# A gated cross-attention and quantized FFN block: quantized tokens transposed on TensorE, a new prologue, another order at the end of block 7, and block 1's queries from transposed tokens in DRAM

## The chip, the core and the metric

One core of one Trainium2 chip runs the program. The metric is the device time of one execution in microseconds. TensorE is called PE here, its weight loads PEld, VectorE DVE, ScalarE ACT, GpSimd POOL, and SyncE, which issues nearly all DMAs, SP. Every engine executes its own instructions in order.

## The reference

There are 2 x 2048 tokens of width 512, a context of 77 tokens for each of the two batches, and 16 heads of width 32. The FFN has 2048 hidden values and rounds its operands to integers, with one scale for a whole tensor.

```python
x = x + tanh(g_xattn) * xattn(layernorm(x), ctx)       # softmax(q k^T / sqrt(32)) v, then Wo, bo
x = x + tanh(g_ffn) * ffn(layernorm(x))

def quant(x):                       # per tensor
    scale = max(max(abs(x)), 1e-6) / 127
    return round(x / scale), scale
def qlinear(x, w, b):
    xq, sx = quant(x); wq, sw = quant(w)
    return (xq @ wq.T + b) * (sw * sx)
ffn(x) = qlinear(gelu(qlinear(x, w1, b1)), w2, b2)
```

## The kernel before

The 4096 tokens are eight blocks of 512 (`TB`), each of four tiles of 128; blocks 0 to 3 belong to batch 0. All eight blocks of x stay in SBUF (`X[i]`). The program has three stages: attention over all blocks, in fp32 (0 to 396 us of the profile); the first product of the FFN over all blocks, in bf16 integers (to 509 us); and the second product (to the end).

**Order.** In the attention the order of every engine's instructions, SP's included, is the order of the program's text (`manual_schedule`). In the first FFN product this holds for PE alone; a scheduler places the rest.

**Attention.** A block has four groups of four heads, and runs in eight steps `s`; a step takes one group and two tiles (`part` gives which). `scores` of a step are made on PE (L528) two steps ahead; DVE takes the maxima (`mx`, L537), ACT the exponentials (`e`, eight instructions, L548); DVE sums (`sm`, L562) and inverts (`rs`), POOL multiplies (`e`, L566), PE transposes (`pta`, L577), ACT copies (`aT`), PE multiplies with V (`pc`, L586; L605 in block 7) and ACT copies (`cT`). Queries of block 0 and 1 come from `project_q` (`pq`, L353), those of later blocks and all output projections from 7 units of products of quarters (`qa`, `qb`, `oa`, `ob`, L443), whose sums of quarters POOL makes (`wq_s`, `wo_t`, `xt`, `cs`, L380). Work of neighbouring blocks is spread over the steps by the tables `begin`, `second`, `plan` and `end`; `at(k, task)` puts a task at the end of global step k = 8 i + s.

**Prologue.** For block 0, x is loaded by tiles; DVE takes statistics and normalizes (`xn`, L335), POOL makes the inverse deviation (`rstd`, L174 and L175), PE transposes (`ptx`, L344), ACT copies (`xnT`). PE projects K by groups (`pk`, L236); DVE places each group in a block matrix (`place_k`: four instructions, with ACT taking half of them in batch 1). `nbk`, a scaled bias that only batch 1 uses, is made on POOL from the load `bk_sb`. `pk`, `pq`, `pvv` (V) and `pm` alternate between two PSUM banks (`bank`), in the order of the text.

**Queries.** In block 1 the tokens are normalized and transposed as in block 0 (steps 2 to 4). From block 2 on, `xT`, a copy of x that is transposed in DRAM, is loaded instead (`load_xT`); POOL multiplies it by a row of rstd (`scale_x`, L306), and Wq has had the mean of its rows taken off (`center_wq`, after `sum_columns`), which does what subtracting the mean of the tokens would. The row goes through DRAM: SP writes it (`write_row`, L293), waits for it and reads it as a row on all partitions (`read_row`, L299).

**Block 7** takes the half of tiles 0 and 1 for all groups first (steps 0 to 3), then the half of tiles 2 and 3 group by group, so that the output projections of tiles 2 and 3 (`project_o`, L621) end only with the last group. The scale of the FFN's input needs the extremes of all rows (`extreme`, L647, on DVE); after it the chain goes over `pg_x` to `xqT0`, the quantized, transposed tokens of block 0.

**First product.** For each block, 16 chunks of hidden values in four tiles `G`: four matmuls of 128x512 each (`ph`, L1031), gelu on ACT (L1039), and a maximum over each two chunks on DVE (`hmax`, L1049). `quantize_x` makes the tokens of the next block: DVE normalizes four tiles, multiplies and rounds in two passes of half a block (`quantize`, L211 and L212), and SP transposes each tile by a DMA:

```python
nc.sync.dma_start_transpose(xqT[:, :, r], xq[:, t, :])      # L1010, four per block
```

22 of the 32 tiles G are written to DRAM, 10 are held. The second product (L1098) follows when the last maximum gave its scale.

Of the kernel before, what the change touches and what calls it, by code (L numbers as in the profile page):

```python
# [42 lines left out]
def tile_flamingo_gated_block(  # L43
# [88 lines left out]
    for g in range(2, NG):  # L132
        load_group(nc.sync, wq_sb, wqT, g)
    for b in range(1, B):
        load_ctx(nc.sync, b)
    load_x(1)
# [5 lines left out]

    nc.sync.dma_start(wo_sb, kchunks(woT))
# [10 lines left out]
    nc.vector.memset(ones, 1.0)  # L154
    mhalf = const.tile([P, NT], F32, name="mhalf")
# [6 lines left out]
    hmax = const.tile([P, NB * GT * 2 + 1], F32, name="hmax")  # L162
# [55 lines left out]
    with actx:  # L218
# [97 lines left out]
        def sum_columns(total):  # L316

            pm = bank("pm")
            nc.tensor.matmul(pm, ones, total, start=True, stop=True)
            mean = work.tile([P, D], F32, tag="rrow", name="wq_mean", bufs=1)  # L320
            nc.scalar.activation(mean, pm, AF.Copy, scale=1.0 / D)
            return mean
# [27 lines left out]
        def project_q(i, g):  # L350
            pq = bank(f"pq{i}_{g}")
            for kc in range(KC):
                nc.tensor.matmul(  # L353
                    pq,
                    wq_sb[:, kc, g * P : (g + 1) * P],
                    (xnT if i < 2 else xT_sb)[i][:, kc, :],
                    start=(kc == 0),
                    stop=(kc == KC - 1),
                )
# [153 lines left out]
        def part(i, s):  # L513


            return divmod(s, 2) if i + 1 < NB else (s % NG, s // NG)

        def scores(i, s):

            g, half = part(i, s)  # L520
# [3 lines left out]
            for u in range(2):  # L524
                t = 2 * half + u
# [71 lines left out]
        def apply_v_half(i, s):  # L597

            g, half = part(i, s)
            odd = s % 2  # L600
            pc = ps_t.tile([P, H], F32, tag="pt", name=f"pc{i}_{s}")
            for j in range(HG):
                r = slice(j * DK, (j + 1) * DK)
                c = g * P + j * DK
                nc.tensor.matmul(  # L605
                    pc[r, :],
                    vblk[i // NBB][:, c : c + DK],
                    aT[i, s // 2][:, j, odd * H : (odd + 1) * H],
                    start=True,
                    stop=True,  # L610
                )
            if s in (0, 2):
                cT[i, g // 2] = work.tile([P, 2, TB], F32, tag="cT", name=f"cT{i}_{g}", bufs=3)
            nc.scalar.copy(cT[i, g // 2][:, g % 2, half * H : (half + 1) * H], pc)
# [135 lines left out]
        begin = {1: ("", "p2"), 3: ("", "p3"), 5: ("", "P0"), 6: ("", "P1"), 7: ("", "P2")}  # L750
# [25 lines left out]
        nbk = small.tile([P, KC], F32, tag="nbk", name="nbk", bufs=1)  # L776
        nc.gpsimd.tensor_scalar(nbk, bk_sb, -SCALE, None, ALU.mult)
# [27 lines left out]
        for i in range(NB):  # L805
# [3 lines left out]
            for s in range(2 * NG):  # L809
# [22 lines left out]
                if i == 0:  # L832
# [7 lines left out]
                    if s in (5, 6):  # L840
                        for n in range(2):
                            sums_wq(2 * (s - 5) + n)
# [5 lines left out]
                if i > 0 and s < 2:  # L848
                    for n in ((1, 2), (4,))[s]:
                        sums_c(i - 1, n)  # L850
                if more and i > 0:
# [5 lines left out]
                for t in range(NT):  # L857
                    if s == ((4, 5, 6, 7) if i == 0 else (4, 4, 5, 6))[t]:
# [15 lines left out]
                if i > 0:  # L874
# [4 lines left out]
                    these = {5: (0,), 6: (1,), 7: (2,)} if more else {6: (0, 1), 7: (2,)}  # L879
# [11 lines left out]
                if not more and s > 4:  # L891

                    if s < 7:
                        project_o(i, s - 5)
                        later = [(add_o, i, s - 5), (norm2_stats, i, s - 5)]
                    else:
                        both = ps_s.tile([P, NR, 512], F32, tag="ps", name="po_last")
                        for these in (0, 1), (2,):
                            project_o(i, 2, these)
                            for n, c in enumerate(halves):  # L900
                                project_o(i, 3, these, c, psum=both[:, n, :])
# [12 lines left out]
                for task, args in tasks.get(k, ()):  # L914
                    task(*args)
                if i + 2 < NB:
# [8 lines left out]
        i, last = NB - 1, range(NG - 1, NG)  # L925
# [4 lines left out]
        project_o(i, 2, last)  # L930
        for c in halves:
            project_o(i, 3, last, c)
        for n in range(3, 2 * NT):
            extreme(i - 1, n)
        for t in range(2):
            norm2_max(i, t)
        add_o(i, 2)
        norm2_stats(i, 2)
        norm2_max(i, 2)
# [50 lines left out]
    with ExitStack() as fctx:  # L990
# [3 lines left out]
        )  # L994

        def quantize_x(i):

            xqT = xqT0
            if i % 2:
                xqT = fwork.tile([P, KC, TB], BF16, tag="xqT", name=f"xqT{i}", bufs=1)  # L1000
            n = NT // 2
            for t0 in range(0, NT, n):
                xs = fwork.tile([P, n, D], F32, tag="xs", name=f"xs{i}_{t0}")
                xq = fwork.tile([P, n, D], BF16, tag="xq", name=f"xq{i}_{t0}")
                for t in range(n):
                    normalize2(xs[:, t, :], i, t0 + t)
                quantize(xq, xs, inv_x)
                for t in range(n):
                    r = slice((t0 + t) * P, (t0 + t + 1) * P)
                    nc.sync.dma_start_transpose(xqT[:, :, r], xq[:, t, :])  # L1010
            return xqT

        fctx.enter_context(tc.manual_schedule(engines={mybir.EngineType.PE}))
        for i in range(NB):
            cur = xqT if i else xqT0
            if i + 1 < NB:
                with tc.issue_after(last):
                    xqT = quantize_x(i + 1)
            for a in range(GT):
                G = gtile(f"G{i}_{a}")  # L1020
                for v in range(GF // 2):
# [24 lines left out]
                    k = (i * GT + a) * 2 + v  # L1046
                    n = 1 if k == NB * GT * 2 - 1 else 2
                    for u in range(0, 2, n):
                        nc.vector.tensor_reduce(  # L1049
                            hmax[:, k + u : k + u + 1],  # L1050
                            G[:, 2 * v + u : 2 * v + u + n, :],
# [136 lines left out]
```

## Time and profile before

| | |
|---|---|
| Time, median of 3 runs | 631.1 us (630.91 to 632.41) |
| The profiled execution | 631.38 us, its span 629.5 us |
| Mean granted clock of PE | 0.991 |
| DMA | 94.95 MB, mean 151 GB/s |
| Attention, first product, second product | 0 to 396.4, 396.4 to 508.7, 513.2 to 626.3 us |

Times in the profile count from the start of the span. An instruction's duration is its own; matmuls are pipelined, so the distance between their starts is what counts, and that is what the chain of waits shows. "x8" counts instructions; an fp32 matmul is two, an fp32 transpose one.

### The profile page before, as it was taken

Reading aid. Unit: us, or ns where it says so; the run is one execution under the profiler, and the core shown is the slowest. Engines: PE = TensorE matmul, PEld = TensorE weight load, DVE = VectorE, ACT = ScalarE, POOL = GpSimd, SP = SyncE. Lnnn points to the kernel's source line nnn. Section 1 sums busy time; section 2 is a strip of 40 time slices with the busy share of each in tenths; the row PEclk is TensorE's granted clock in tenths of the full one; section 3 lists DMA queues with packets and bytes.
Section 4 is the critical chain, followed back from the end, with each engine's and each line's share of the span. In section 5 each row is a group of like instructions: output and inputs, shape, how many; then the busy total and the mean of one; then the engine's idle time right before and its main releaser. Section 6 shows DMA issues by size and latency. Waiting matters only on the chain.

```text
span 629.5 us, 9452 instructions
## 1 busy us (share of the span) xinstructions
PE 596.9 (95%) x3322; PEld 370.1 (59%) x3322; DVE 478.3 (76%) x743; ACT 411.3 (65%) x926; POOL 330.6 (53%) x291
## 2 busy tenths in 40 slices
PE   3999999899999999999999997899999979999997
PEld 3556467677778777777777744344444424444444
DVE  4476658668998788778666868999999789877452
ACT  1377556777766867866766653698999879555620
POOL 3076687679777799697885462000000009997000
PEclk9999999999999999999999999799999989999999
DMA  9910350041360053240000040399998019798932
GB/s 288 374 54 1 135 133 18 1 151 67 134 218 1 18 180 124 84 168 1 17 1 1 2 151 0 108 334 342 342 345 232 1 60 376 272 367 320 399 127 83
DMA packets 51270, 94.95 MB, mean 151 GB/s; under 512 B 22219, under 2 KB 26571, under 8 KB 45464
## 3 DMA queue, kind: packets, MB, share of 16 engines
q1 hardware_dynamic: 50120, 93.67, 43.6%
q10 hardware_dynamic: 1104, 0.69, 0.4%
q8 instruction: 26, 0.43, 0.3%
q14 instruction: 20, 0.16, 0.2%
HBM read 57.11 MB, written 33.57 MB: 144 GB/s over the span
## 4 chain that ended last, share of the span: by engine, by line
PE 80%; DVE 9%; ACT 4%; POOL 4%; issue 1%; DMA 1%; ACTq 0%; POOLq 0%; DVEq 0%
PE ph L1031 18%; PE pf L1098 17%; PE pta L577 8%; PE oa L443 6%; PE ps L528 5%; PE qa L443 5%; PE ob L443 5%; PE qb L443 4%; PE pc L586 3%; PE pq L353 3%; ACT e L548 2%; PE po L621 2%; PE pvv L261 1%; POOL cs L380 1%; DVE sm L562 1%
## 5 line engine op out<-in xcount | busy, mean ns | idle before, releaser
L566 POOL TENSOR_TENSOR e<-e,rs 128x616 f32<-128x616 f32 x64 | 77.8, 1216 | 95.7 <-DVE rs L564 89.3
L548 ACT ACTIVATE e<-ps,mx 128x77 f32<-128x77 f32 x512 | 116.9, 343 | 9.9 <-DVE mx L537 9.7
L1098 PE MATMUL pf<-w2q,hq 128*128 128x512 bf16 (+1 forms) x528 | 112.4, 376 | 2.5 <-DVE hq L212 2.3
L1031 PE MATMUL ph<-xqT,w1q 128*128 128x512 bf16 x512 | 112.4, 383 | 1.8 <-DVE xqT L212 1.8
L1039 ACT ACTIVATE G<-ph,b1s,s 128x512 f32<-128x512 f32 x128 | 99.2, 777 | 13.6 <-PE ph L1031 2.9
L578 ACT COPY aT<-pta 77x512 f32<-77x512 f32 x128 | 68.8, 587 | 53.4 <-PE pta L577 53.4
L1098 PEld LDWEIGHTS <-hq 128*128 128x128 bf16 x528 | 51.8, 98 | 63.0 <-DVE hq L212 3.1
L1031 PEld LDWEIGHTS <-w1q 128*128 128x128 bf16 x512 | 50.5, 99 | 63.6 <-issue 4.3
L1049 DVE TENSOR_REDUCE hmax<-G 128x1 f32<-128x1024 f32 (+1 forms) x65 | 76.9, 1197 | 7.0 <-ACT G L1039 6.9
L577 PE MATMUL pta<-ident,e 128*77 128x128 f32 x512 | 71.2, 281 | 2.9 <-POOL e L566 1.3
L1089 POOL TENSOR_SCALAR b_sb<-b_sb,s 128x512 f32<-128x512 f32 x1 | 3.5, 3493 | 122.1 <-issue 122.1
L562 DVE TENSOR_REDUCE sm<-e 128x8 f32<-128x616 f32 x64 | 50.4, 787 | 22.7 <-ACT e L548 22.5
L537 DVE TENSOR_REDUCE mx<-ps 128x8 f32<-128x616 f32 x64 | 50.2, 785 | 22.7 <-PE ps L528 22.5
L1091 ACT ACTIVATE Gb<-Gb,inv_h 128x2048 f32<-128x2048 f32 x22 | 43.6, 2000 | 31.9 <-DMA Gb<-h 30.8
L577 PEld LDWEIGHTS pta<-ident,e 128*77 128x77 f32 x512 | 55.5, 147 | 14.8 <-issue 8.0
L528 PEld LDWEIGHTS ps<-kb,qT 64*128 64x128 f32 x512 | 36.0, 186 | 37.1 <-issue 31.4
L1112 POOL TENSOR_TENSOR x<-x,b_sb 128x512 f32<-128x512 f32 x32 | 57.2, 1825 | 0.1
L528 PE MATMUL ps<-kb,qT 64*128 64x154 f32 x512 | 50.6, 317 | 0.7 <-DVE qT L489 0.4
L1120 DVE SCALAR_TENSOR_TENSOR x<-pf,s,x 128x512 f32<-128x512 f32 (+1 forms) x33 | 23.7, 729 | 34.6 <-PE pf L1098 26.8
L647 DVE TENSOR_REDUCE xm<-x 128x1 f32<-128x512 f32 x64 | 40.8, 669 | 0.0
L348 POOL TENSOR_TENSOR x<-x,bo_sb 128x512 f32<-128x512 f32 x32 | 40.4, 1272 | 0.0
L1092 DVE TENSOR_SCALAR hq<-Gb 128x2048 bf16<-128x2048 f32 x22 | 36.5, 1701 | 1.2 <-ACT Gb L1091 1.1
(146 smaller groups left out, 939.9 us busy)
## 6 DMA issues: line engine op xcount, KB each, us to landing
h<-G SPq DMA_DIRECT2D x22, 1024.0 KB, 5.2
Gb<-h SPq DMA_DIRECT2D x22, 1024.0 KB, 7.8
out_y<-x SPq DMA_DIRECT2D x31, 256.0 KB, 3.1
x<-in_x SPq DMA_DIRECT2D x7, 1024.0 KB, 6.9
xT<-in_xT SPq DMA_DIRECT2D x6, 1024.0 KB, 9.0
raw_w<-in_w2T SPq DMA_DIRECT2D x6, 1024.0 KB, 6.6
raw_w<-in_w1T SPq DMA_DIRECT2D x4, 1024.0 KB, 12.5
w_dram<-xqT SPq DMA_DIRECT2D x4, 512.0 KB, 3.3
```

The costliest lines, as they stand in the source:

```text
L443: nc.tensor.matmul(ps[:, m * H : (m + 1) * H], a[:, c, m * P : (m + 1) * P], b[:, c, :], start=(m + c == 0 and not more), stop=(m + c == 2 ...
L528: nc.tensor.matmul(ps[:, q, u * RK : (u + 1) * RK], qT[i, g // 2][r, g % 2, t * P : (t + 1) * P], kblk[i // NBB][r, g, :], start=True, sto ...
L548: last = nc.scalar.activation(es[i, s][:, u, j * NK : (j + 1) * NK], sc[:, q, u, r, :], AF.Exp, bias=mx[:, q, u, r : r + 1], scale=-1.0,)
L562: nc.vector.tensor_reduce(sm, e4, AX.X, ALU.add)
L566: return nc.gpsimd.tensor_tensor(e4, e4, rs[:, :, :, None].to_broadcast([P, 2, HG, NK]), ALU.mult).ins
L577: nc.tensor.transpose(pt[:NK, j, :], es[i, s][:, u, j, :], ident)
L578: nc.scalar.copy(aT[i, g][:, :, t * P : (t + 1) * P], pt[:NK, :, :])
L1031: nc.tensor.matmul(ph[u], w1q[:, kc, fc * P : (fc + 1) * P], cur[:, kc, :], start=(kc == 0), stop=(kc == KC - 1),)
L1039: nc.scalar.activation(G[:, 2 * v + u, :], ph[u], AF.Gelu, bias=b1s[:, fc : fc + 1], scale=s1,)
L1049: nc.vector.tensor_reduce(hmax[:, k + u : k + u + 1], G[:, 2 * v + u : 2 * v + u + n, :], AX.XY, ALU.max, apply_absolute_value=True,)
L1098: nc.tensor.matmul(po[t, c.start][:, : c.stop - c.start], hq[:, fc, t * P : (t + 1) * P], w2q[:, fc, c], start=(fc == 0), stop=(fc == FC - 1),
L1112: nc.gpsimd.tensor_tensor(y, y, b2_sb, ALU.add)
```

## The change

`quantize_x` no longer transposes by DMA. DVE folds the scale into one pass (`rq`) and rounds in one more; PE transposes the bf16 tiles by `ident16` ahead of the matmuls of tiles a = 2 and a = 3 (`transpose_q`, 8 transposes each), and ACT copies the first half, DVE the second. There is one maximum for each G but the last.

In the prologue 24 transposes of the identity are put ahead of and behind the first transposes, `nbk` goes behind the normalization, K's groups 1 to 3 are placed after the first two scores, and the loads of x1 and the new xT1 come earlier; the fourth piece of w1 is loaded at step 5. Block 1 takes its queries from `xT`: its row is written at step 1, `center_wq` moves from step 3 to step 2, `scale_x` stands at step 3, and all of batch 1's K and V come in steps 3 and 4. Additions of bo (`add_bias`) in blocks 0 and 1 and a sum of Wq move to later steps.

In block 7 the second half goes by tiles: steps 4 and 5 take tile 2, 6 and 7 tile 3, each with two groups. The eight extremes of block 6 move from the end to steps 4 and 5.

```diff
+    load_x(1)
     for g in range(2, NG):
         load_group(nc.sync, wq_sb, wqT, g)
     for b in range(1, B):
         load_ctx(nc.sync, b)
-    load_x(1)
+    load_xT(1)
     nc.sync.dma_start(wo_sb, kchunks(woT))
...
+    ident16 = const.tile([P, P], BF16, name="ident16")
+    nc.vector.tensor_copy(ident16, ident)
...
-        def part(i, s):
-            return divmod(s, 2) if i + 1 < NB else (s % NG, s // NG)
+        def part(i, s, u):
+            if i + 1 < NB:
+                return s // 2, 2 * (s % 2) + u
+            return (s, u) if s < NG else (2 * (s % 2) + u, s // 2)
...
-        begin = {1: ("", "p2"), 3: ("", "p3"), 5: ("", "P0"), 6: ("", "P1"), 7: ("", "P2")}
+        begin = {1: ("", "p2"), 2: ("", "p3"), 5: ("", "P0"), 6: ("", "P1"), 7: ("", "P2")}
...
-        nbk = small.tile([P, KC], F32, tag="nbk", name="nbk", bufs=1)
-        nc.gpsimd.tensor_scalar(nbk, bk_sb, -SCALE, None, ALU.mult)
+        run_up = ps_s.tile([P, KC, P], F32, tag="ps", name="run_up")
+        for n in range(21):
+            nc.tensor.transpose(run_up[:, n % KC, :], ident, ident)
         pk = {}
         for t in range(NT + 1):
...
                 normalize(0, t - 1)
                 transpose_x(0, t - 1)
+            if t == 1:
+                for n in range(3):
+                    nc.tensor.transpose(run_up[:, n, :], ident, ident)
             if t in (2, 3):
                 pk[t - 2] = project_k(0, t - 2)
+        nbk = small.tile([P, KC], F32, tag="nbk", name="nbk", bufs=1)
+        nc.gpsimd.tensor_scalar(nbk, bk_sb, -SCALE, None, ALU.mult)
         place_k(0, 0, pk[0])
-        pk[2] = project_k(0, 2)
-        place_k(0, 1, pk[1])
         project_q(0, 0)
-        place_k(0, 2, pk[2])
-        pk[3] = project_k(0, 3)
-        place_k(0, 3, pk[3])
         load_x(2)
-        for j in range(4):
+        for j in range(3):
             load_w("w1", j)
+        at(5, load_w, "w1", 3)
         for s in range(2):
             scores(0, s)
             exponential(0, s)
+        place_k(0, 1, pk[1])
+        for g in range(2, NG):
+            place_k(0, g, project_k(0, g))
         project_q(0, 1)
...
+                    if s == 3:
+                        for kc in range(KC):
+                            scale_x(1, kc)
...
-                    if s == ((4, 5, 6, 7) if i == 0 else (4, 4, 5, 6))[t]:
+                    if s == ((5, 5, 6, 6) if i == 0 else (5, 6, 6, 7) if i == 1 else (4, 4, 5, 6))[t]:
                         add_bias(i, t)
...
-                if i == 0 and s in (2, 3):
-                    normalize(1, 2 * s - 4)
-                    normalize(1, 2 * s - 3)
...
-                    these = {5: (0,), 6: (1,), 7: (2,)} if more else {6: (0, 1), 7: (2,)}
+                    these = {5: (0,), 6: (1,), 7: (2,)} if more else {4: (0, 1, 2, 3), 5: (4, 5, 6, 7)}
                     for n in these.get(s, ()):
                         extreme(i - 1, n)
...
                 if i == 0 and s == 2:
-                    mean = sum_columns(total)
-                if i == 0 and s == 3:
-                    center_wq(mean)
+                    center_wq(sum_columns(total))
                 if i == 0 and s in (3, 4):
-                    transpose_x(1, 2 * s - 6)
-                    transpose_x(1, 2 * s - 5)
-                if i == 0 and 3 <= s < 7:
                     for b in range(1, B):
-                        place_k(b, s - 3, project_k(b, s - 3))
-                        if s == 6:
+                        for n in ((0, 1, 2), (3,))[s - 3]:
+                            place_k(b, n, project_k(b, n))
+                        if s == 4:
                             project_v(b)
...
+                if k == 1:
+                    write_row(1)
+                    at(k + 1, read_row, 1)
...
-        def quantize_x(i):
...
-                quantize(xq, xs, inv_x)
-                for t in range(n):
-                    r = slice((t0 + t) * P, (t0 + t + 1) * P)
-                    nc.sync.dma_start_transpose(xqT[:, :, r], xq[:, t, :])
+        rq = const.tile([P, NB, NT], F32, name="rq")
+        with tc.issue_after(last):
+            nc.vector.tensor_scalar(rq, rstd2, inv_x, None, ALU.mult)
+        HT = NT // 2
+        def quantize_x(i, half):
+            xs = fwork.tile([P, HT, D], F32, tag="xs", name=f"xs{i}_{half}")
+            xq = fwork.tile([P, HT, D], BF16, tag="xq", name=f"xq{i}_{half}")
+            for u in range(HT):
+                t = half * HT + u
+                nc.vector.tensor_scalar(
+                    xs[:, u, :], X[i][:, t, :], mean2[:, i, t, 0:1], rq[:, i, t : t + 1],
+                    ALU.subtract, ALU.mult,
+                )
+            nc.vector.tensor_scalar(xq, xs, MAGIC, MAGIC, ALU.add, ALU.subtract)
+            return xq
+        def transpose_q(xqT, i, half, xq):
+            r = slice(half * HT * P, (half + 1) * HT * P)
+            pt = ps_q.tile([P, KC, HT, P], BF16, tag="pq", name=f"ptq{i}_{half}")
+            for u in range(HT):
+                for kc in range(KC):
+                    nc.tensor.transpose(pt[:, kc, u, :], xq[:, u, kc * P : (kc + 1) * P], ident16)
+            pt = pt.rearrange("p k u t -> p k (u t)")
+            if half:
+                nc.vector.tensor_copy(xqT[:, :, r], pt)
+            else:
+                nc.scalar.copy(xqT[:, :, r], pt)
...
                 G = gtile(f"G{i}_{a}")
+                if a >= 2 and i + 1 < NB:
+                    transpose_q(xqT, i + 1, a - 2, xq[a - 2])
```

More of the change, by code (lines that the diff above doesn't have):

```diff
@@ L319, in sum_columns @@
             nc.tensor.matmul(pm, ones, total, start=True, stop=True)
[L320 removed]
+            mean = work.tile([P, D], F32, tag="xn", name="wq_mean")
             nc.scalar.activation(mean, pm, AF.Copy, scale=1.0 / D)
@@ L524, in scores @@
             for u in range(2):
-                t = 2 * half + u
+                g, t = part(i, s, u)
                 for q in range(NR):
@@ L597, in apply_v_half @@
         def apply_v_half(i, s):
-            g, half = part(i, s)
             odd = s % 2
[L601 to L611, printed above, removed]
+            (g, t), (g1, t1) = part(i, s, 0), part(i, s, 1)
+            pc = ps_t.tile([P, 2, P], F32, tag="pt", name=f"pc{i}_{s}")
+            a = aT[i, s // 2][:, :, odd * H : (odd + 1) * H]
+            for n, group in enumerate([g] if g == g1 else [g, g1]):
+                tokens = slice(0, 2) if g == g1 else slice(n, n + 1)
+                for j in range(HG):
+                    c = group * P + j * DK
+                    nc.tensor.matmul(
+                        pc[j * DK : (j + 1) * DK, tokens, :],
+                        vblk[i // NBB][:, c : c + DK],
+                        a[:, j, tokens.start * P : tokens.stop * P],
+                        start=True,
+                        stop=True,
+                    )
             if s in (0, 2):
                 cT[i, g // 2] = work.tile([P, 2, TB], F32, tag="cT", name=f"cT{i}_{g}", bufs=3)
-            nc.scalar.copy(cT[i, g // 2][:, g % 2, half * H : (half + 1) * H], pc)
+            if g == g1:
+                nc.scalar.copy(cT[i, g // 2][:, g % 2, :H], pc.rearrange("p u t -> p (u t)"))
+            else:
+                nc.scalar.copy(cT[i, g // 2][:, :, t * P : (t + 1) * P], pc)
         def project_o(i, t, groups=range(NG), c=ALL, psum=None):
@@ L923, in tile_flamingo_gated_block @@
                         at(k + 2, read_row, i + 2)
-        i, last = NB - 1, range(NG - 1, NG)
+        i, last = NB - 1, range(NG - 2, NG)
         apply_v_half(i, 2 * NG - 1)
```

84 lines of the change are left out of this document (43 added, 41 removed).

## The prediction

> **What bounds the kernel now.** I read the busy table first, then stretches of the run by engine, the chain that ended last, and the issue times of SP.
>
> ```profile
> PE 596.9 (95%) x3322; PEld 370.1 (59%) x3322; DVE 478.3 (76%) x743; ACT 411.3 (65%) x926; POOL 330.6 (53%) x291
> ```
>
> TensorE (PE) is busy for 596.9 of 629.5 us, so only 32.6 us can be won by removing waits; any instruction added to PE where it never waits is paid in full. Busy time by stretch (start:end, length, then PE, PEld, DVE, ACT and POOL with their counts, and the granted clock):
>
> ```profile
> 0.00:22.60 22.60, 12.32 (x56) 10.00 (x56) 8.92 (x25) 4.30 (x6) 5.81 (x18) 1.00 0.97 310
> 22.60:61.00 38.40, 35.65 (x203) 20.75 (x202) 24.24 (x44) 25.61 (x84) 20.83 (x18) 1.00 0.30 111
> 104.00:146.00 42.00, 39.65 (x252) 29.66 (x244) 31.02 (x58) 31.66 (x86) 32.83 (x29) 1.00 0.19 57
> 146.00:344.00 198.00, 196.98 (x1270) 150.94 (x1272) 158.24 (x283) 138.33 (x434) 154.31 (x139) 1.00 0.24 81
> 370.00:396.40 26.40, 19.68 (x97) 10.97 (x96) 22.14 (x50) 9.60 (x23) 9.84 (x18) 0.94 0.17 72
> 410.00:452.00 42.00, 42.00 (x196) 19.02 (x195) 42.00 (x53) 37.78 (x50) 0.00 (x0) 1.00 1.05 330
> ```
>
> The waits lie at the start (10.3 us), in block 0 (2.8), around blocks 1 and 2 (2.4) and at the end of attention (6.7). From 146 to 344 PE idles 1 us, so whatever is won earlier is kept. In the first product of the FFN (last row) PE never waits. It runs 396.40 to 508.75: 512 matmuls in 112.35 us, of which the first 3.4 us at granted clock 0.50 lose 1.7, so one costs 0.216.
>
> The start, in the chain of waits (start, duration, what):
>
> ```profile
> 2.14 6.08 DMA bk_sb<-in_bk
> 8.30 0.23 POOL nbk L777
> 8.93 0.58 POOL rstd L175
> 9.54 0.55 DVE xn L335
> 14.13 0.85 PE ptx L344 x4
> 14.99 1.62 PE pk L236 x8
> 22.74 1.25 PE ps L528 x16
> 31.05 0.72 PE ps L528 x8
> ```
>
> POOL's `nbk` waits for a small load and holds up the rstd of block 0 behind it. Four transposes cost 0.85 here and a K group 1.62. In the timeline a K group takes 1.01 at 21.7, and eight transposes take 1.04 (0.13 each) at 387: PE is slow until about 17.
>
> SP's issues of the rstd row, to DRAM and back:
>
> ```profile
> 116.74 0.37 SPq L293 DMA_DIRECT2D row<-rstd  x1
> 125.12 0.34 SPq L299 DMA_DIRECT2D rrow<-row  x1
> ```
>
> The read waits for the write: 8.4 us here, 8.3 to 12.0 over the six rows, and the read lands 3.3 to 5.9 us after its issue.
>
> **The change, part by part.** The profiled execution took 631.38 us around its span of 629.5; the median of the runs is 631.1, 0.3 lower. About 0.3% (1.9 us) is what a measurement of this kernel can tell from no change.
>
> *Prologue.* `nbk` goes behind the rstd. DVE then normalizes tile 0 when stats, variance and rstd are done: the second stats end at 5.6, the bf16 identity adds 0.3 (128x128, row `diag_w`), so 5.9 instead of 9.5; tile 3 ends at 10.3 instead of 13.9. The 24 run-up transposes (0.21 each cold, 5.1 us) fill PE's idle time from 2.0 on. If they bring the clock up by about 8, pk_0, ptx_2, pk_1 take 1.0, 0.5, 1.0, ptx_3 ends at 11.5, its copy at 12.2, pq_0 takes 3.45, its copy 0.7: first scores at 16.5 instead of 22.7. If not, two pk and three ptx cost 0.6 and 0.33 more each: 18.7.
>
> *K groups behind the scores.* Then 4.4 us are given back. `bank` has two buffers: pk_2 waits for pk_1 to be placed, pq_1 for pk_2. From the first scores T: the two maxima end at T+2.3, kb_1 (four times 0.3) at T+3.5, pk_2 at T+4.5, kb_2 at T+5.8; pq_1 runs to T+9.3 and pvv to T+12.7, where ps_2 starts. Before, pk_2 and pk_3 filled the waits for the xnT and qT copies and ps_2 came at T+8.3. So ps_2 starts at 29.2 instead of 31.0: **-1.8** (+0.5 if cold). Each placement is queued on DVE behind the two maxima, and the first sum of e behind all; POOL's e_0 at T+9.3 is still early for PE at T+13.4.
>
> *Block 1's tokens.* Out: 16 transposes (2.1 us of PE), 4 normalizations on DVE (0.9 each), 4 copies on ACT. In, on POOL: 4 scalings (1.33 each), and centering one step earlier. PE's waits of 3.8 us between ps_2 and the end of pta_7 at 75.9, most from those normalizations and placements, shrink to 2.8: half of it is pk_2 of batch 1, whose bank is freed by ACT's placements, queued behind eight exponentials. With the 2.1 that is -3.1; but POOL now stops at the scalings. Counting from pq_2 (35.1 before), rstd is ready at +7.9 (41.9 plus 1.0 in the trace), the row is back 8.3 to 12.0 plus 3.3 to 5.9 us later, at +19.5 to +25.8; POOL arrives at +17.9. Queued behind are e_5, then e_6 and the additions; PE wants e_5 at +24.9 (pta_5), and gets it after 5.3 of scaling and 1.2 of e_5, at +26.0 to +32.3. Loads are over by then, so I take +27.6, nearest to the rows with idle DMA: 2.7 of wait, so -3.1 + 2.7 = **-0.4** (-2.0 to +4.3).
>
> On SP, x1 and the new xT1 (1 MB each, 2.7 us at 374 GB/s) stand ahead of weights first needed 10 us after landing; the fourth w1 piece was held by its buffer until 70.6 anyway. Nothing, unless the rows find SP waiting for a slot.
>
> *Block 1.* Two additions of bo (2.49 us on POOL at 108.3) leave their place ahead of e_6 and xt_2, for which PE waits 1.62 at 114.2: **-1.6** (0 if another engine is as late there). They go where POOL idles 4.6 and 2.8 us.
>
> *Block 7.* With tile 2 complete early, the final DVE queue holds 6 extremes (0.6 each) instead of 10 plus 2. The last additions start at 388.1 rather than 389.4: -1.3. The eight extremes of block 6 now stand between maxima and sums of steps 4 and 5 and delay e_7 by 0.3: **-1.0** (-1.5 to +1).
>
> *FFN.* 28 DMA transposes (median 3.1 us to land) leave SP. PE never waited for one, so this frees nothing; nor does DVE's saving of 14 passes of 0.74. PE gains 7 x 16 = 112 transposes with a weight load each. Floor 0.054 (128 of 512 columns at 0.216), ceiling 0.107 (128x256 matmuls with own load: 16 between the last two additions, 624.66 to 626.34). I take 0.07, near the floor, since the fp32 transposes, with twice the bytes to load, need 0.13: 112 x 0.07 = **+7.8** (6.0 to 12.0). Their covers hold: xq is made a block ahead; per block ACT has 12.4 + 1.1 (copy of 128x1024, twice 0.59) and DVE about 13.9 (four reductions of 2.28, estimated from 0.68 and 1.21 for a quarter and a half of it, four normalizations of 0.54, two roundings of 0.7, a copy of 1.2), against PE's 14.9.
>
> [...]
>
> **Sum:** -1.8 - 0.4 - 1.6 - 1.0 + 7.8 = +3.0, so 631.4 + 3.0 - 0.3 = **634.1**.
>
> **Rivals.** *The run-up doesn't raise the clock:* +2.3, 636.4. For it: in the trace PE was busy with transposes and pk from 11.4 and got fast only at 17. Against: transposes made up half of that.
>
> *The weight load paces the transposes at 0.105:* 11.8 instead of 7.8, 638.1. For it: LDWEIGHTS bf16 is 98 ns long. Against: it lies hidden under 107 ns matmuls without a gap, so its issue may be shorter.
>
> *Not slower: the lead of 6.2 us at the first scores is kept.* Place: the two banks. If kb_1 and kb_2 slip in such that pq_1 starts 2.6 us after the first scores instead of 5.8, 3.2 us more are won: 630.9; it decides if ps_2 starts by 26. With the transposes at their floor as well, 629.1. Against: DVE's order puts both maxima ahead of kb_1.
>
> **How the numbers follow.** Forecast 0.43, cold start 0.20, paced by loads 0.15, lead kept 0.22. The range 629.5 to 638.8 goes from the lead kept at a floor price to beyond the load-paced case. Slower by over 0.3% (above 633.0): 0.35 + 0.20 + 0.15 = 0.70; within: 0.08 + 0.12 = 0.20; faster: 0.10.
>
> **What would show it.** Right: the first ph to the last ph takes 8 us longer, ptq at 0.07 each, no wait of PE on xq; first scores near 16.5 and ps_2 near 29; POOL's first xT scaling waits for DMA `rrow`, and pta_5 of block 0 for POOL; no wait at xt_2 in block 1. Wrong: ps_2 at 26 or before, POOL's scaling without a wait, or an FFN that is no longer than before.

## The result, and the profile after

| | before | after |
|---|---|---|
| Median of 11 runs each | 631.48 us (630.91 to 632.87) | 636.06 us (634.47 to 639.43) |
| The profiled execution, its span | 631.38, 629.5 us | 639.43, 637.6 us |
| Mean granted clock of PE in it | 0.991 | 0.979 |
| First FFN product begins / its length | 396.40 / 112.35 | 396.37 / 119.88 |
| Second product begins / its length | 513.16 / 113.14 | 521.39 / 113.14 |

The ratio of the medians is 1.0069, interval 1.0055 to 1.0083: 4.6 us slower, where +3.0 was forecast and the range reached to 638.8. The profiled execution happens to be the longest of the eleven, 3.4 us above the median. Its granted clock accounts for that. A stretch of 3.41 us at half clock costs 1.7 us, half of it, where PE is busy throughout; the profile has eight such stretches (three before), and the clock of the runs around the median, 0.983, stands for six (0.017 of 634 us, 1.7 us for each).

In what follows pk_2 is the projection of K's group 2 and kb_2 its placement, pq_1 the queries of group 1, pvv batch 0's V; ps_2 are the scores of step 2, e_5 the exponentials of step 5 after POOL's multiplication, and pta_5 their transposes, all of block 0 where no other is named.

First the busy row and the clock row of the page after:

```profile
PE 610.9 (96%) x3474; PEld 381.8 (60%) x3474; DVE 467.9 (73%) x703; ACT 414.8 (65%) x929; POOL 335.3 (53%) x296
...
PEclk9798899999999999999999999899999979999999
```

PE is busy for 14 us more, in 152 instructions more: 112 bf16 transposes and the 24 of the run-up came, 16 fp32 ones left, the products with V in block 7's second half are 64 of 128 columns instead of 32 of 256, and part of the work ran at half clock. DVE is busy 10 us less, ACT 3.5 and POOL 4.7 more. The clock row has dips in slices 2, 4 and 5 (16 to 32 and 48 to 80 us), where the kernel before had none. The same stretches as before, in the same columns (start:end, length, PE, PEld, DVE, ACT, POOL with counts, granted clock, DMA share, GB/s):

```profile
0.00:22.60 22.60, 16.55 (x93) 13.38 (x94) 10.02 (x27) 7.88 (x22) 6.20 (x19) 0.94 1.00 320
22.60:61.00 38.40, 36.08 (x174) 20.81 (x174) 17.32 (x40) 20.55 (x65) 19.90 (x17) 0.90 0.52 173
104.00:146.00 42.00, 40.81 (x256) 30.66 (x255) 32.15 (x60) 31.56 (x91) 32.77 (x31) 1.00 0.17 57
146.00:344.00 198.00, 196.99 (x1265) 151.63 (x1264) 159.40 (x284) 138.64 (x433) 155.96 (x139) 1.00 0.26 81
370.00:396.40 26.40, 21.23 (x127) 12.53 (x128) 21.64 (x49) 10.85 (x25) 10.84 (x19) 0.98 0.21 83
410.00:452.00 42.00, 42.00 (x232) 20.49 (x231) 36.56 (x34) 37.33 (x49) 0.00 (x0) 1.00 0.69 280
```

The clock column of the first row says nothing of the very start: before, it shows 1.00 although a K group took 1.62 us there. In the second row PE is busy 0.4 us longer than before with 29 instructions fewer, at a mean clock of 0.90. That is the surprise of this case. In the last row PE is still full, now with 36 instructions more (48 transposes, and 12 matmuls fewer), and DVE has fallen from 42.0 to 36.6, which moved nothing.

PE in the first scores of the profile after, from the timeline (start, duration, what, and in brackets the idle time before it):

```profile
16.25 1.32 PE L533 MATMUL ps<-kb,qT 64*128 64x154 f32 x16 [0.78 <-ACT qT L367]
19.94 3.54 PE L240 MATMUL pk<-ctx,wk_sb 128*128 128x77 f32 x16 [2.38 <-issue]
23.28 5.45 PE L357 MATMUL pq<-xnT,wq_sb 128*128 128x512 f32 x8
28.57 3.60 PE L265 MATMUL pvv<-wv_sb,ctx 128*77 128x512 f32 x8
32.09 0.79 PE L533 MATMUL ps<-kb,qT 64*128 64x154 f32 x8
```

The first scores start at 16.25 (16.5 was predicted), and PE then waits 2.38 us for the bank of pk_2, as predicted. But the two K groups behind the wait take 3.3 us instead of 2.0 and pq_1 5.3 instead of 3.5 (2.0 and 3.5 as in the run with a filled wait below). Three pairs of neighbouring stretches show why (the next to last but one column is the granted clock):

```profile
16.68:20.09 3.41, 1.03 (x16) 0.83 (x12) 2.68 (x6) 2.17 (x11) 0.00 (x0) 1.00 1.12 364
20.09:26.92 6.83, 6.83 (x21) 4.76 (x22) 3.35 (x10) 1.40 (x7) 0.96 (x1) 0.50 1.00 368
50.81:54.23 3.42, 2.19 (x18) 1.28 (x20) 1.50 (x6) 1.77 (x7) 2.84 (x3) 1.00 0.00 0
54.23:57.64 3.41, 3.41 (x19) 3.10 (x20) 1.76 (x3) 1.76 (x4) 0.00 (x0) 0.50 0.66 100
61.05:64.47 3.42, 1.48 (x10) 0.56 (x8) 2.53 (x4) 0.00 (x0) 3.42 (x4) 1.00 0.62 237
64.47:67.88 3.41, 3.05 (x10) 2.45 (x11) 3.34 (x7) 1.58 (x4) 3.41 (x4) 0.50 0.00 0
```

Each time PE is idle for 1.2 to 2.4 us of a stretch of 3.41 us, and the next one or two stretches are granted half the clock. The change's three waits in block 0 (for pk_2's bank, for the third K group of batch 1, for e_5) each did this once.

The chain of waits through block 0 is the one that was predicted (start, duration, what):

```profile
43.12 1.06 POOL rstd L179
...
44.19 8.09 DMA row<-rstd
...
52.30 6.24 DMA rrow<-row
...
59.89 3.71 POOL xT L310 x3
63.60 1.18 POOL e L571
...
64.83 1.99 PE pta L582 x8
```

The row is back 14.3 us after its write, POOL scales, e_5 follows, and PE has waited 2.30 us for it.

### The profile page after: what moved, and what is told of

It is laid out like the page before. It is cut to its first block, busy times and chain, and to the rows that moved or that the text cites. A ratio compares the mean times of both kernels' runs of the same rounds, so it can differ in the third digit from the quotient of the medians.

```text
span 637.6 us, 9656 instructions
## 1 busy us (share of the span) xinstructions
PE 610.9 (96%) x3474; PEld 381.8 (60%) x3474; DVE 467.9 (73%) x703; ACT 414.8 (65%) x929; POOL 335.3 (53%) x296
## 4 chain that ended last, share of the span: by engine, by line
PE 79%; DMA 7%; DVE 5%; POOL 4%; ACT 3%; SPq 1%; issue 1%; ACTq 0%; POOLq 0%; DVEq 0%
PE pf L1139 18%; PE ph L1068 17%; PE pta L582 8%; PE oa L447 7%; PE qa L447 5%; PE ps L533 5%; PE ob L447 5%; PE pc L591 4%; PE qb L447 4%; PE pq L357 2%; DMA raw_w<-in_w1T 2%; PE po L631 2%; DMA wo_sb<-in_woT 1%; ACT e L553 1%; DMA row<-rstd 1%; POOL cs L384 1%
## 5 line engine op out<-in xcount | busy, mean ns | idle before, releaser
L1068 PE MATMUL ph<-xqT,w1q 128*128 128x512 bf16 x512 | 115.9, 386 | 1.8 <-DVE xqT L216 1.8
L1068 PEld LDWEIGHTS <-w1q 128*128 128x128 bf16 x512 | 50.2, 99 | 61.1 <-issue 5.9
L1090 DVE TENSOR_REDUCE hmax<-G 128x1 f32<-128x2048 f32 (+2 forms) x34 | 73.0, 2155 | 14.9 <-ACT G L1076 14.9
L582 PE MATMUL pta<-ident,e 128*77 128x128 f32 x512 | 72.6, 285 | 3.5 <-POOL e L571 2.9
L542 DVE TENSOR_REDUCE mx<-ps 128x8 f32<-128x616 f32 x64 | 50.2, 786 | 32.9 <-PE ps L533 32.7
L582 PEld LDWEIGHTS pta<-ident,e 128*77 128x77 f32 x512 | 57.0, 150 | 14.7 <-issue 8.3
L310 POOL TENSOR_TENSOR xT<-xT,rrow 128x512 f32<-128x512 f32 x28 | 36.9, 1340 | 5.0 <-DMA rrow<-row 5.0
```

What stands on the lines that cost most here:

```text
L582: nc.tensor.transpose(pt[:NK, j, :], es[i, s][:, u, j, :], ident)
L1068: nc.tensor.matmul(ph[u], w1q[:, kc, fc * P : (fc + 1) * P], cur[:, kc, :], start=(kc == 0), stop=(kc == KC - 1),)
L1090: nc.vector.tensor_reduce(hmax[:, k + n : k + n + 1], G[:, part_of, :], AX.XY, ALU.max, apply_absolute_value=True,)
```

## The experiments

All times are medians. Each ratio is to runs of the kernel before beside them, whose medians were 631.2 to 631.7. The diffs show the core of each edit; "..." stands where lines are left out.

**1. The FFN alone, and the attention alone.** The first run takes the kernel before with `transpose_q`, `rq` and the whole-G maxima; the second is the changed kernel with the old `quantize_x` and DMA transposes.

```diff
# attention alone, against the changed kernel
-                if a >= 2 and i + 1 < NB:
-                    transpose_q(xqT, i + 1, a - 2, xq[a - 2])
+                    nc.sync.dma_start_transpose(xqT[:, :, r], xq[:, t, :])
```

> The kernel before with only the first FFN product changed: bf16 transposes on TensorE instead of by DMA, the folded scale, one maximum for each G. Theory: in the trace of the changed kernel eight transposes push the next matmul back by 0.45 us, so 112 cost 112 x 0.056 = 6.3 us; the longer maximum ahead of the last chunks lengthens the way from the last matmul of the first product to the first of the second from 4.4 to 5.1 us (0.7). So 631.5 + 7.0 = 638.5 (637 to 640). First rival, the price that I predicted (0.07 each): 631.5 + 7.8 + 0.7 = 640. Second rival, the DMA transposes and DVE passes that go away give something back: 635 or less.

> The changed kernel with the first FFN product as before (DMA transposes), so that only the attention differs from the kernel before. Theory: 636.1 - 7.0 = 629.1 (627.5 to 631): the attention's changes are worth about -2.4 in the median run, because waits in block 0 set the granted clock to 0.5 for 2 to 4 stretches of 3.4 us, each of which costs 1.7 us; first FFN matmul at about 394. Rival: they are worth nothing (the profiled run of the changed kernel starts the FFN at 396.37 against 396.40): 631.5. Second rival, my sum without any clock loss: 631.5 - 4.8 = 626.7.

Measured: FFN alone 637.95, ratio 1.0094 (1.008 to 1.0108), so +6.4. Attention alone 630.05, ratio 0.9972 (0.9961 to 0.9983), so -1.5. The one is the whole loss and more, and the other is a third of the gain that was forecast. The timeline of PE in the FFN-only run gives the price of a transpose:

```profile
404.89 0.61 PE L1031 MATMUL ptq<-ident,xq 128*128 128x128 bf16 x8
405.33 3.62 PE L1061 MATMUL ph<-xqT,w1q 128*128 128x512 bf16 x15
408.79 0.61 PE L1031 MATMUL ptq<-ident,xq 128*128 128x128 bf16 x8
409.24 2.97 PE L1061 MATMUL ph<-xqT,w1q 128*128 128x512 bf16 x13
```

From the first of eight to the next matmul it is 0.44 to 0.45 us, 0.056 each: the floor of 0.054, a quarter of the 0.216 us that 512 columns cost. 112 of them are 6.3 us. What DVE and SP were spared gave nothing back. Behind the product a small loss appears that the prediction did not have: the way from the last `ph` to the first `pf` grows from 4.41 to 4.84 us, because DVE's queue at the end holds a whole maximum more. In the changed kernel's DVE timeline it starts at 513.64 and, with the pieces of the last G behind it, lasts

```profile
513.64 4.60 DVE L1090 TENSOR_REDUCE hmax<-G 128x1 f32<-128x2048 f32 x4 [1.17 <-ACT G L1076]
```

up to 2.0 us after the last `ph`, where the kernel before was done 1.5 us after it.

**2. The waits filled.** If the clock is lost by PE's idle time, useless work in the wait should keep it. One run puts 17 transposes of the identity ahead of pk_2, another fills all three waits.

```diff
+        def fill(name, n):
+            pf = ps_t.tile([P, KC, P], F32, tag="pt", name=f"fill{name}")
+            for m in range(n):
+                nc.tensor.transpose(pf[:, m % KC, :], ident, ident)
...
         place_k(0, 1, pk[1])
+        fill(0, 17)
         for g in range(2, NG):
             place_k(0, g, project_k(0, g))
```

> The changed kernel with 17 more transposes of the identity (0.13 us each, 2.2 us) on TensorE where it waits 2.4 us for a bank ahead of pk_2. They compute nothing that is used. Theory: that wait drops the granted clock to 0.5 for 6.8 us (20.1 to 26.9 in the profile); transposes count as work for the clock, so it stays at 1.0, pk_2 still starts near 19.9, pq_1 takes 3.6 instead of 5.4 and ps_2 starts near 28.7 instead of 32.1: 636.1 - 3 = 633 (632 to 635). Rival: the clock isn't decided by that wait, or transposes don't count for it: 636.1, and if the fill reaches past the wait 0.5 more.

> As the run before, with 12 more transposes ahead of the third K group of batch 1 (wait of 1.7 us at 50.3) and 17 ahead of the transposes of e_5 in block 0 (wait of 2.3 us at 62.5). Theory: with all three waits filled no stretch of clock 0.5 is left between 17 and 390 us, another 1.7 to 3.4 us against the run with one fill: 631 (629.5 to 632.5), and block 0's pta_7 ends at 74 to 75 instead of 78.6. Rival: the waits themselves and not the clock cost the time: the same as with one fill, or up to 1.5 slower where a fill is longer than its wait.

Measured: 634.15, ratio 1.0043 (1.0028 to 1.0058), with one fill; 634.45, ratio 1.0044 (1.0029 to 1.0059), with three. PE in the run with one fill:

```profile
16.44 1.32 PE L533 MATMUL ps<-kb,qT 64*128 64x154 f32 x16 [0.78 <-ACT qT L367]
17.69 2.07 PE L790 MATMUL fill<-ident 128*128 128x128 f32 x17
20.14 1.98 PE L240 MATMUL pk<-ctx,wk_sb 128*128 128x77 f32 x16 [0.38 <-issue]
22.59 3.67 PE L357 MATMUL pq<-xnT,wq_sb 128*128 128x512 f32 x8 [0.47 <-PE pk L240]
26.09 3.60 PE L265 MATMUL pvv<-wv_sb,ctx 128*77 128x512 f32 x8
29.62 0.79 PE L533 MATMUL ps<-kb,qT 64*128 64x154 f32 x8
```

pk_2 starts no earlier, and yet everything behind it takes what it takes at full clock; ps_2 comes at 29.62 instead of 32.09. 17 instructions that compute nothing won 1.9 us. The clock and the DMA share of the same two stretches in this run:

```profile
16.05:19.46 3.41, 3.02 (x32) 2.86 (x33) 2.12 (x5) 1.68 (x8) 0.00 (x0) 1.00 1.07 367
19.46:26.29 6.83, 5.98 (x28) 3.65 (x27) 3.91 (x12) 2.20 (x11) 1.22 (x1) 1.00 1.02 349
```

The loads run as densely as in the changed kernel (1.12 and 1.00 there), so they are not what made pk_2 and pq_1 slow; the clock is what differs. With three fills no stretch between 10 and 390 us is at half clock, but the time is the same: pta_5 starts at 62.10 against 62.02, because e_5 comes from POOL behind the row (first with one fill, then with three):

```profile
62.02 1.10 PE L582 MATMUL pta<-ident,e 128*77 128x128 f32 x8 [0.42 <-POOL e L571]
62.10 1.10 PE L582 MATMUL pta<-ident,e 128*77 128x128 f32 x8 [1.78 <-POOL e L571]
```

So the half clock from 50.2 to 57.0 us in the run with one fill was hidden by the row's wait, and my expectation of 631 for the run with three fills failed: the lost clock cost nothing where POOL and not PE set the pace.

**3. Without the run-up.** The 24 transposes are left out; nothing else differs from the changed kernel.

```diff
-        for n in range(21):
-            nc.tensor.transpose(run_up[:, n % KC, :], ident, ident)
...
-            if t == 1:
-                for n in range(3):
-                    nc.tensor.transpose(run_up[:, n, :], ident, ident)
```

> The changed kernel without the 24 run-up transposes. Theory: TensorE is at half clock until 13 to 17 us, first scores near 18.7 instead of 16.3, which is the 2.3 us of the prediction's cold case; the wait ahead of pk_2 is still there, so the clock may be lost again right after: 638 (637 to 639). Rival: transposes don't count for the clock, the run-up does nothing, first scores at 16.3 without it: 636.1. Second rival: half of what it wins is given back at pta_5, where the row of rstd decides: 637.

Measured: 640.43, ratio to the kernel before 1.0131 (1.0097 to 1.0165), 4.4 us slower than the changed kernel and above the 637 to 639 expected. PE's timeline:

```profile
12.86 1.06 PE L348 MATMUL ptx<-ident,xn 128*128 128x128 f32 x4
14.59 5.22 PE L357 MATMUL pq<-xnT,wq_sb 128*128 128x512 f32 x8 [0.68 <-ACT xnT L349]
20.59 1.32 PE L533 MATMUL ps<-kb,qT 64*128 64x154 f32 x16 [0.78 <-ACT qT L367]
```

The first scores come at 20.59 instead of 16.25. The cold case that I had priced at 2.3 us costs 4.3 there, 1.5 of it because pq_0 too runs slowly for most of its length (5.22 us instead of 3.70).

**4. K's groups in their old place.** In the changed kernel pk_2 goes back ahead of pq_0, and pk_3 and all placements ahead of the first scores.

```diff
         place_k(0, 0, pk[0])
+        pk[2] = project_k(0, 2)
+        place_k(0, 1, pk[1])
         project_q(0, 0)
+        place_k(0, 2, pk[2])
+        pk[3] = project_k(0, 3)
+        place_k(0, 3, pk[3])
...
-        place_k(0, 1, pk[1])
-        for g in range(2, NG):
-            place_k(0, g, project_k(0, g))
```

> The changed kernel with K's groups in the place that they had before (pk_2 ahead of pq_0, pk_3 behind it, all placed ahead of the first scores). Theory: pk_2 and pk_3 again fill TensorE's waits for the copies, pq_1 waits for no bank, no wait of more than 1 us is left between 12 and 33 us, so the granted clock stays at 1.0; first scores near 17.5, ps_2 at 26 to 27 (32.1 in the changed kernel's profile, 29.6 with the filled wait), and the row of rstd moves ahead with it: 636.1 - 5 = 631 (630 to 632.5). Rival: block 0 is bound by the row of rstd, whose write is held by loads that don't move; pta_5 stays near 62 and all that is won at ps_2 is given back there: 634 to 635.

Measured: 631.49, ratio 0.9996 (0.9982 to 1.0011), 4.6 us faster than the changed kernel. The first scores are a microsecond later (17.32), the clock stays at 1.0 until 47.6 us, and

```profile
18.57 3.70 PE L357 MATMUL pq<-xnT,wq_sb 128*128 128x512 f32 x8
22.11 3.60 PE L265 MATMUL pvv<-wv_sb,ctx 128*77 128x512 f32 x8
25.63 0.79 PE L533 MATMUL ps<-kb,qT 64*128 64x154 f32 x8
```

ps_2 starts 6.5 us earlier. Of these 6.5, 5.8 are left at pta_5 (59.06 against 64.83), where PE now waits 3.03 us for the row. The groups moved behind the scores were therefore the costliest single step of the change outside the FFN.

**5. Block 1's queries as before.** Its tokens are normalized and transposed, centering and K as in the kernel before, all else as changed.

```diff
-                    (xT_sb if i else xnT)[i][:, kc, :],
+                    (xnT if i < 2 else xT_sb)[i][:, kc, :],
...
-                    if s == 3:
-                        for kc in range(KC):
-                            scale_x(1, kc)
...
+                if i == 0 and s in (2, 3):
+                    normalize(1, 2 * s - 4)
+                    normalize(1, 2 * s - 3)
...
+                if i == 0 and s in (3, 4):
+                    transpose_x(1, 2 * s - 6)
+                    transpose_x(1, 2 * s - 5)
```

> The changed kernel with block 1's queries as before: tokens normalized on DVE and transposed on TensorE, centering a step later, K and V of batch 1 over four steps. Theory: the transposes cost 2.1 us of TensorE and the old waits 1 us, the row's wait of 2.3 us and the cold clock after it (1.7) are gone: about no difference, 636 (635 to 637), as the stretch from ps_2 to the end of pta_7 is 44.9 us in the kernel before, 45.0 in the run with the attention alone and 46.7 in the changed kernel's profile. Rival: the tokens from DRAM win their 3.1 us and the wait costs little: 638 to 639. Second rival: the row's wait is the loss: 633.

Measured: 637.05, ratio 1.008 (1.0058 to 1.0102), 1.0 us slower than the changed kernel. The two intervals (1.0055 to 1.0083 for the changed kernel) overlap for most of their length, so this run can't say whether the tokens from DRAM gained nothing, the 0.4 of the prediction's sum, or a microsecond.

**6. The row earlier.** Block 1's statistics move ahead of block 0's V, where DVE idles, and the row is written and read at once.

```diff
         shares(0, 0)
+        for t in range(NT):
+            norm_stats(1, t)
+        write_row(1)
+        read_row(1)
         project_v(0)
...
-                if i == 0 and s in (0, 1):
-                    norm_stats(1, 2 * s)
-                    norm_stats(1, 2 * s + 1)
...
-                if k == 1:
-                    write_row(1)
-                    at(k + 1, read_row, 1)
```

> The changed kernel with block 1's statistics ahead of block 0's V instead of in steps 0 and 1, and its row of rstd written and read at once; nothing else differs. Theory: DVE idles from 25.8 to 32.2 and x1 is there, rstd is ready at about 31 instead of 44, the row is back by 46 to 50, ahead of POOL's arrival at scale_x (53.7), so POOL no longer waits 5.0 us, e_5 is ready by 60, TensorE's wait of 2.3 us at pta_5 goes, and with it the clock loss behind it where there is one (1.7): 633.3 (632 to 634.5). Rival: block 0 is bound by something else within a microsecond (POOL's 4.9 us of scaling, the placements of batch 1, the clock after the wait at 50): 636 to 636.5.

Measured: 634.08, ratio 1.003 (1.0014 to 1.0046), 2.0 us faster than the changed kernel. SP's issues and POOL's scaling in it:

```profile
30.86 0.37 SPq L297 DMA_DIRECT2D row<-rstd  x1
43.72 0.34 SPq L303 DMA_DIRECT2D rrow<-row  x1
...
53.24 4.93 POOL L310 TENSOR_TENSOR xT<-xT,rrow 128x512 f32<-128x512 f32 x4
```

Under the loads the write takes 12.9 us (8.1 in the changed kernel), but it has the time. POOL scales at once, where it waits 5.01 us in the changed kernel, and PE's wait at pta_5 is gone.

**7. Together.** The first of these kernels also spread batch 1's K as two groups in step 3, two in step 4 and V in step 5; the second left K as in the change (three groups in step 3, one and V in step 4); the third adds 12 transposes of the identity ahead of the third group. All four have DMA transposes and K of block 0 in its old place, the first three the early row. The fourth has block 1's queries as in the kernel before instead of the early row, and no fill.

```diff
# first: batch 1's K and V
-                        for n in ((0, 1, 2), (3,))[s - 3]:
+                        for n in ((0, 1), (2, 3), ())[s - 3]:
...
-                        if s == 4:
+                        if s == 5:
                             project_v(b)
# third: the fill
                         for n in ((0, 1, 2), (3,))[s - 3]:
+                            if n == 2:
+                                fill(1, 12)
                             place_k(b, n, project_k(b, n))
```

> The kernel with the changed attention and the first FFN product as before (DMA transposes), and in it K's groups in their old place, block 1's row early, and K of batch 1 as two groups in step 3, two in step 4 and V in step 5. Theory: no wait over 1 us is left in blocks 0 and 1, no clock loss between 9 and 388 us: 630.05 - 3 (start) - 2.5 (row) = 624.5 (623 to 626.5). Rival: with the start earlier POOL or ACT becomes the bound of block 0 and half of it is lost: 627 to 628.

> The changed attention with the first FFN product as before, K's groups in their old place and block 1's row early; batch 1's K as in the change (three groups in step 3). Theory: the gains of the single runs add up, since the one removes the wait at pk_2 and the other the wait at pta_5: 630.05 - 4.6 - 3.0 = 622.5 (621 to 624), pta_5 near 56 without a wait; the wait of 1.7 us ahead of the third K group of batch 1 stays, and with it 3.4 us or more at half clock. Rival: POOL (4.9 us of centering and 4.9 of scaling in a row) is the next bound within a microsecond: 625.5.

> As the run before, with 12 transposes of the identity in TensorE's wait ahead of the third K group of batch 1. Theory: now that no row decides at pta_5, the clock kept at 1.0 there is worth its 1.7 to 3.4 us: 620 (618.5 to 621.5), no stretch at half clock between 9 and 384 us. Rival: POOL or the placements decide, as in the changed kernel, where three fills won no more than one: 622.5.

> As the kernel with the mended attention (DMA transposes, K's groups in their old place), but block 1's queries as in the kernel before: normalized on DVE, transposed on TensorE, batch 1's K and V over four steps. Theory: with the row early the tokens from DRAM are worth the 3.1 us that the prediction gave them by themselves (2.1 of transposes, 1 of waits), so this is 3 us slower than the better of the two mended kernels: 623 to 623.5. Rival: its evenly spread K groups have no wait that loses the clock, and it is as fast: 620 to 622.5.

Measured: 626.34, ratio 0.9912 (0.9883 to 0.9941); 622.76, ratio 0.9852 (0.9827 to 0.9877); 620.80, ratio 0.9831 (0.9805 to 0.9857); 624.17, ratio 0.9878 (0.9855 to 0.99).

The gains add up, and the third kernel beats both the one before and the changed one, by 10.4 and some 15 us. The first stayed inside its expectation but 1.8 us above its middle, and 3.6 above the second kernel, for a reason that its two stretches show:

```profile
45.59:49.01 3.42, 1.74 (x18) 1.70 (x16) 2.09 (x4) 2.17 (x5) 3.42 (x4) 1.00 0.94 301
49.01:59.25 10.24, 9.26 (x32) 6.35 (x31) 5.63 (x12) 6.23 (x23) 9.69 (x9) 0.50 0.28 103
```

With one K group fewer in step 3, PE came to pta_4 1.68 us before e_4, which stands on POOL behind 4.95 us of centering; three stretches at half clock followed. The fill in the third kernel is worth 2.0 us now that no row hides it. The second kernel's profile has the same wait of 1.70 us at 45.6, but there it falls across two stretches:

```profile
41.36:44.77 3.41, 2.54 (x24) 2.39 (x22) 0.90 (x2) 2.99 (x11) 3.41 (x3) 1.00 0.07 5
44.77:48.19 3.42, 2.58 (x24) 1.67 (x24) 1.89 (x6) 1.77 (x7) 2.46 (x3) 1.00 0.79 140
48.19:55.01 6.82, 6.29 (x36) 3.41 (x34) 3.17 (x7) 4.03 (x13) 5.54 (x5) 1.00 0.75 276
```

Neither has more than 0.87 us of idle time, and the clock is kept; the six runs of this kernel go from 620.99 at a mean clock of 0.991 to 623.54 at 0.986. The filled kernel has 0.991 to 0.993 in all of its runs. Against it, block 1's old queries (624.17, above the 623 to 623.5 expected) cost 3.4 us; against the second kernel's median they cost 1.4, and against its two runs at a clock of 0.991, which is also that of the fourth, 3.1. That agrees with the 3.1 that the prediction gave to the tokens from DRAM by themselves.

## Why the prediction was right, and where it was not

Slower was right, and so was the range; the predicted 634.1 lies 2 us below the median. That it lies so near is in part luck, since transposes priced 1.5 us too dear stood in for some of the clock's cost, which the sum did not have. By its own steps, in the two profiles:

- *Prologue, -1.8 forecast.* ps_2 at 32.09 against 30.98 is **+1.1**. The sequence was as worked out (first scores 16.25, a bank wait of 2.4, kb_1 before pk_2), but the step "pk_2 at T+4.5 ... pq_1 runs to T+9.3" took the durations at full clock behind a wait that had just been counted. With the clock held by the fill ps_2 came at 29.62, where 29.2 was forecast. This is the step that failed, and 2.5 us of it.
- *Block 1's tokens, -0.4 (-2.0 to +4.3).* From ps_2 to the end of pta_7 it took 46.7 us against 44.9: **+1.8**, inside the bounds. The row was back 22.4 us after pq_2 began (19.5 to 25.8), e_5 was ready at +28.6 (27.6 taken) and the wait was 2.30 (2.7). Of the 2.2 us above the forecast 1.0 is this later e_5. The rest lies behind pta_5, where the half clock, which the sum did not have, cost 1.5: from pta_5 to the end of pta_7 it took 13.95 us, and 12.47 with one fill, where the clock was whole. With one fill the stretch from ps_2 took 44.9, no gain where 0.4 was forecast. That the tokens by themselves are worth some 3.1, hidden by the row, is what the mended kernels point to.
- *Block 1, -1.6.* **-1.2**: the wait for xt_2 fell from 1.62 to 0.46 us. The additions of bo left, but POOL still makes e_6 and xt_2 in that order just ahead.
- *Block 7, -1.0.* **-1.75**: 1.45 up to the last addition, and nothing was lost in steps 4 and 5. The 0.3 behind it is not the change's: the two matmuls of `pg_x` fell into a half-clock stretch before (0.79 us) and not after (0.49).
- *FFN, +7.8.* **+7.5** in the profile, right for a wrong reason: 6.3 for the transposes, at 0.056 rather than 0.07, and 1.3 because the product ran at half clock for 6.0 us at its start instead of 3.4. The fp32 row (0.13) that held the estimate off the floor had no bearing on bf16.
- *Between the products, nothing forecast.* **+0.7** in this profile. 0.43 of it, the whole of it in the FFN-only run, comes from the longer maximum at the end of DVE's queue; the other 0.3 is `pg_h`, whose two matmuls at 518.84 took 0.80 us at half clock, against 0.49 before. I had looked at DVE's share of a block but not at its last instructions.

The wait for xt_2 in block 1 after the change:

```profile
115.94 1.99 PE L447 MATMUL qa<-xt,wq_s 128*128 128x256 f32 x8 [0.46 <-POOL xt L384]
```

The steps are +1.1 + 1.8 - 1.2 - 1.75 + 7.5 + 0.7 = 8.1, the difference of the spans. The median run, by its clock, has two stretches of half clock fewer.

Of the rivals, the useless run-up is refuted: without the run-up the first scores come 4.3 us later. Transposes paced at 0.105 are refuted by 0.056. The lead was kept once K stood in its old place: ps_2 at 25.6 ("by 26") and 631.49, where 630.9 was worked out.

Transposes counted for the clock here, both in raising it (a K group takes 1.01 us at 8.26 behind the run-up, 1.83 at 8.76 without it) and in keeping it (1.00 in the two stretches from 19.46 us behind the filled wait, 0.50 in the two from 20.09 behind the empty one). A bf16 transpose is recorded as 0.219 us long, and took 0.056 from start to start.

## What to carry to other kernels

In this kernel a new wait on TensorE had two prices: its length, and the clock behind it (2.4 us and 2.5 us at pk_2). When an order is changed so that PE waits a microsecond or more, ask what runs next at half clock and whether it is PE that sets the pace there; then move other PE work into the wait, and only if there is none fill it. A step that is moved off its old place must also be asked what it was covering there: pk_2 and pk_3 filled the waits for two copies, and the third K group of batch 1 hid the centering.

## What was not expected of the hardware

- The granted clock changes in stretches of 3.41 us, and idle time far shorter than that is enough. In the attention of the kernel before and of the changed kernel, from 9 us on, each stretch at full clock with 1.94 us of idle time or more was followed by half clock (1.94 and 2.38 in block 0, 2.92 and 3.40 at the end), and none with 1.10 (at 113.12 us before) or less. Between, both occur: 1.23 us (from 50.81 in the changed kernel) and 1.68 (from 45.59 in the first kernel of experiment 7) led to half clock, and a wait of 3.03 us that fell as 1.81 and 1.22 into two stretches (from 54.43, with K's groups in their old place) kept the clock. What decides there, the kind of the matmuls around the wait or something else, is open.
- Where a stretch falls against the program differs from profile to profile: around the first scores one begins at 16.68 us in the changed kernel, at 16.05 with one fill. A wait of 1.68 us in one stretch was followed by three at half clock, a wait of 1.70 across two (0.87 and 0.84 us of idle time) by none. That this also sets apart runs of one kernel (620.99 at a clock of 0.991 and 623.54 at 0.986) is my estimate. The changed kernel's runs spread over 5.0 us, and those of the kernel with the filled wait and no other long one lie, five of six, within 0.7. The clock is not the whole of the spread: the sixth of these took 622.66 at 0.992, and the changed kernel took 634.47 and 637.71 at the same 0.986. What these runs lost is not shown.
- A stretch at half clock in which PE was busy throughout, by its records, was not always the last one. In the changed kernel (from 20.09) and without the run-up (from 24.51) it held little but K groups of 77 columns, and another followed; in the attention-only run (from 51.71), with one fill (50.18) and with the early row (53.05) it held products with V and scores, and another followed too. In the changed kernel from 54.23 and with K's groups in their old place from 47.60, scores and transposes filled it, and the clock was back after one; so it was in the attention-only run from 20.99, with K groups and queries. What decides is open.
